# Layer 3's forward transform recorded in a fixed order of all engines, with products one group ahead, channels innermost, and other slots for layer 2

## The chip, the core and the metric

The kernel runs on one core of a Trainium2 chip. The metric is the device time of one execution in microseconds (us), from the first to the last instruction. The engines are named as the profile names them: PE multiplies matrices, PEld is its loading of weights (it runs beside PE), DVE works on vectors, ACT copies and applies functions, POOL is the general engine, SP issues most of the loads. SBUF is the memory that the engines read; PSUM takes the results of PE.

## The reference, cut to what matters

Four layers follow each other on x of 4 x 64 x 256 x 256 (images, channels, rows, columns), each of them x + f(norm(x)) with a norm over groups of two channels. The change touches the last layer, and the slots in SBUF that layer 2 takes over from layer 1.

```python
# layer 3: a few Fourier modes of the normalized x, mixed over channels
x_ft = jnp.fft.rfft2(x)
top = jnp.einsum('bixy,ioxy->boxy', x_ft[:, :, :M1, :M2], w1)       # M1 = M2 = 16
bot = jnp.einsum('bixy,ioxy->boxy', x_ft[:, :, H - M1:, :M2], w2)
out_ft = jnp.zeros((B, Co, H, Wf), dtype=x_ft.dtype)
out_ft = out_ft.at[:, :, :M1, :M2].set(top)
out_ft = out_ft.at[:, :, H - M1:, :M2].set(bot)
return jnp.fft.irfft2(out_ft, s=(H, W))

# ... cut: layers 0 to 2
x = x + _L1_conv_ref(_gn(x), L1_conv_kernel)      # 3x3 convolution
x = x + _L2_conv_ref(_gn(x), ...)                 # differences to neighbours, mask, two products
x = x + _L3_conv_ref(_gn(x), L3_conv_weights1, L3_conv_weights2)
```

## The kernel before

All data are float32. Three kinds of slots of one size (`y0`, `y1`, `y2`, two buffers each) live through all layers. Each is 11 x 258 floats in each of 128 partitions, and each layer takes them in its own way.

```python
def slot(self, k, name):
    return self.slots.tile([128, 11, self.W + 2], F32, tag=f"y{k}", name=name)
```

Layer 1 keeps its input tiles in `y0` and `y1` in turn, and its two normalized tiles in `y2`. Its loop, all engines in recorded order:

```python
xns = [self.slot(2, f"xn1_{k}")[:, 0:10] for k in range(2)]
# ... in load(n):
x = xt[n] = self.slot(n % 2, f"x1_{n}")[:, 0:10, 0:W]
# ... in normalize(n):
x, xn = xt.pop(n), xns[n % 2]
# ... the loop, NI = 64 blocks of 16 rows
for n in range(NI):
    load(n + 3)
    product(n, 1)
    fetch(n)
    product(n, 2)
    finish(n - 1)
    transform(n + 1, 1, 2)
    middle(n)
    product(n, 0)
    result(n, 0)
    transform(n + 1, 0, 3)
    normalize(n + 2)
    product(n, 3)
    result(n, 3)
    self.next_norms()
    ts.pop(n)
finish(NI - 1)
```

`normalize` is an ACT operation (line 256, `xn <- x, nb, r`), `fetch` an ACT copy (line 860, `s <- m`), `transform` are DVE operations (line 842, `t <- xn`), `middle` and `result` are DVE sums (lines 866 and 872), and `finish` takes sums for the next norm on ACT (lines 884 and 888, `junk <- o`).

Layer 2 begins with its slots and its first loads; block n, half g takes the input slot ((2n + g) mod 3) mod 2 and the normalized tile (2n + g) mod 3:

```python
xns = [self.slot(k, f"xn2_{k}_{i}")[:, 0:10] for i, k in enumerate((1, 2, 2))]
z = p_z.tile([128, 2, 10, W + 2], F32, name="z")
for t in xns + [z[:, 0], z[:, 1]]:
    nc.gpsimd.memset(t[:, :, 0 : W + 2 : W1], 0.0)
its = [(b, r0) for b in range(B) for r0 in range(0, H, 32)]
# ... cut
def load(n, g, s, ins=None):
    if n >= NI:
        return
    b, r0 = its[n]
    if s == 0:
        xt[n, g] = self.slot(((2 * n + g) % 3) % 2, f"x2_{n}_{g}")[:, 0:10, 0:W]
    top = r0 + 16 * g + 8 * s - 1
    i0, i1 = max(0, -top), min(10, H - top)
    d = nc.sync.dma_start(xt[n, g][halves[s], i0:i1], src[b][:, top + i0 : top + i1, :])
    if ins:
        self.after(d, ins)
for n, g in ((0, 0), (0, 1), (1, 0)):
    for s in range(2):
        load(n, g, s)
# ... cut: constants, then load_r (line 1004): the residual rows, eight loads each
```

The forward part of layer 3 takes four channels of an image at a time (a group, 1.05 MB, one load into a slot). It multiplies along the rows (`psa`), copies the result to SBUF on ACT (`a`), transposes it on PE (`psat`), and collects it with DVE in `ah`. After 16 groups of an image it multiplies along the width (`psx`), copies (`xw`), transposes again (`psxt`), and spreads the result over `xm`, scaled by the norm:

```python
for b in range(B):
    ah = p_ah.tile([128, NW, C, 4 * M], F32, tag="ah", name=f"ah_{b}")
    for c0 in range(0, C, CC):
        x = first.pop(c0, None) if b == 0 else None
        x = xs[b, c0] = x or load(b, c0, f"x3_{b}_{c0}")
        for c1 in range(0, CC, 4):
            ps = ps_a.tile([128, 2, W], F32, tag="a", name=f"psa_{b}_{c0}_{c1}")
            for n in range(NH):
                for j in range(2):
                    nc.tensor.matmul(
                        ps[halves[j]], eh[:, n, :], x[:, c1 + 2 * j : c1 + 2 * j + 2, n, :],
                        start=(n == 0), stop=(n == NH - 1),
                    )
            m = p_a.tile([128, 2, W], F32, tag="m", name=f"a_{b}_{c0}_{c1}")
            nc.scalar.copy(m, ps)
            pt = ps_t.tile([128, NW, 2, 2, 4 * M], F32, tag="t", name=f"psat_{b}_{c0}_{c1}")
            for n in range(NW):
                for k in range(2):
                    nc.tensor.transpose(
                        pt[:, n, k].rearrange("p j f -> p (j f)"),
                        m[:, k, n * 128 : (n + 1) * 128], self.ident,
                    )
            c = c0 + c1
            for n in range(NW):
                nc.vector.tensor_copy(
                    ah[:, n, c : c + 4, :].rearrange("p (j k) f -> p k j f", j=2), pt[:, n]
                )
        if c0 % 16 == 0:
            self.next_norms()
    if b < 3:
        load_w(b * NK)
    psx = ps_x.tile([128, 4, 128], F32, tag="x", name=f"psx_{b}")
    ahv = ah.rearrange("p n c (s g k r) -> p n g r k s c", s=2, g=4, k=4)
    for n in range(NW):
        for ri in range(2):
            for g in range(4):
                nc.tensor.matmul(
                    psx[32 * g : 32 * g + 32].rearrange("p k (s c) -> p k s c", s=2),
                    ew[:, n, ri, :], ahv[:, n, g, ri],
                    start=(n == 0 and ri == 0), stop=(n == NW - 1 and ri == 1),
                    tile_position=(0, 32 * g),
                )
    xw = p_a.tile([128, 4, 128], F32, tag="m", name=f"xw_{b}")
    nc.scalar.copy(xw, psx)
    pxt = ps_x.tile([128, 2, 4, 4, 2, M], F32, tag="xt", name=f"psxt_{b}")
    for s in range(2):
        for k in range(4):
            for h in halves:
                nc.tensor.matmul(
                    pxt[h, s, k].rearrange("p g r w -> p (g r w)"), xw[:, k, s * C : (s + 1) * C],
                    self.ident, start=True, stop=True,
                )
    r, nb = self.r[3][:, b : b + 1], self.nb[3][:, b : b + 1]
    up, low = halves
    for s in range(2):
        xb = xm[:, s, :, :, :, b].rearrange("p (g k) w r -> p k g w r", g=4)
        for k in range(4):
            v = pxt[:, s, k].rearrange("p g r w -> p g w r")
            nc.vector.tensor_scalar(xb[up, k], v[up], r[up], None, ALU.mult)
            nc.vector.tensor_scalar(xb[low, k, :, :, 0], v[low, :, :, 1], r[low], -1.0, ALU.mult, ALU.mult)
            nc.vector.tensor_scalar(xb[low, k, :, :, 1], v[low, :, :, 0], r[low], None, ALU.mult)
    for k, h in enumerate(halves):
        dc = xm[h, 0, 0, 0, k, b : b + 1]
        nc.vector.scalar_tensor_tensor(dc, nb[h], float(H * W), dc, ALU.mult, ALU.add)
```

Here the scheduler chooses the order of instructions on each engine. After that follow the mixing of the modes (`psm <- xm, wt`, line 1325, 1024 short PE records, weights in eight loads of 2.1 MB, of which `load_w` above starts the first three) and the inverse part (loads of x again, products, sums, stores).

Of the kernel before, what the change touches and what calls it, by code (L numbers as in the profile page):

```python
# [118 lines left out]
class _Net:  # L119
# [812 lines left out]
    def _layer2(self, ctx, src, dst):  # L932
# [18 lines left out]
        xns = [self.slot(k, f"xn2_{k}_{i}")[:, 0:10] for i, k in enumerate((1, 2, 2))]  # L951
        z = p_z.tile([128, 2, 10, W + 2], F32, name="z")
        for t in xns + [z[:, 0], z[:, 1]]:
            nc.gpsimd.memset(t[:, :, 0 : W + 2 : W1], 0.0)
# [16 lines left out]
        for n, g in ((0, 0), (0, 1), (1, 0)):  # L971
            for s in range(2):
                load(n, g, s)
        ones = cp.tile([128, Q], F32, name="ones")
# [227 lines left out]
    def _layer3(self, ctx, src, dst):  # L1202
# [33 lines left out]
        with ExitStack() as c2:  # L1236
# [11 lines left out]
            for b in range(B):  # L1248

                ah = p_ah.tile([128, NW, C, 4 * M], F32, tag="ah", name=f"ah_{b}")  # L1250
                for c0 in range(0, C, CC):
                    x = first.pop(c0, None) if b == 0 else None
                    x = xs[b, c0] = x or load(b, c0, f"x3_{b}_{c0}")
                    for c1 in range(0, CC, 4):
                        ps = ps_a.tile([128, 2, W], F32, tag="a", name=f"psa_{b}_{c0}_{c1}")
                        for n in range(NH):
                            for j in range(2):
                                nc.tensor.matmul(  # L1258
                                    ps[halves[j]], eh[:, n, :], x[:, c1 + 2 * j : c1 + 2 * j + 2, n, :],
                                    start=(n == 0), stop=(n == NH - 1),  # L1260
                                )
                        m = p_a.tile([128, 2, W], F32, tag="m", name=f"a_{b}_{c0}_{c1}")
                        nc.scalar.copy(m, ps)  # L1263
                        pt = ps_t.tile([128, NW, 2, 2, 4 * M], F32, tag="t", name=f"psat_{b}_{c0}_{c1}")
                        for n in range(NW):
                            for k in range(2):
                                nc.tensor.transpose(  # L1267
                                    pt[:, n, k].rearrange("p j f -> p (j f)"),
                                    m[:, k, n * 128 : (n + 1) * 128], self.ident,
                                )  # L1270
                        c = c0 + c1
                        for n in range(NW):
                            nc.vector.tensor_copy(
                                ah[:, n, c : c + 4, :].rearrange("p (j k) f -> p k j f", j=2), pt[:, n]
                            )
                    if c0 % 16 == 0:
                        self.next_norms()
                if b < 3:
                    load_w(b * NK)

                psx = ps_x.tile([128, 4, 128], F32, tag="x", name=f"psx_{b}")
                ahv = ah.rearrange("p n c (s g k r) -> p n g r k s c", s=2, g=4, k=4)
                for n in range(NW):
                    for ri in range(2):
                        for g in range(4):
                            nc.tensor.matmul(  # L1286
                                psx[32 * g : 32 * g + 32].rearrange("p k (s c) -> p k s c", s=2),
                                ew[:, n, ri, :], ahv[:, n, g, ri],
                                start=(n == 0 and ri == 0), stop=(n == NW - 1 and ri == 1),
                                tile_position=(0, 32 * g),  # L1290
                            )
                xw = p_a.tile([128, 4, 128], F32, tag="m", name=f"xw_{b}")
                nc.scalar.copy(xw, psx)

                pxt = ps_x.tile([128, 2, 4, 4, 2, M], F32, tag="xt", name=f"psxt_{b}")
                for s in range(2):
                    for k in range(4):
                        for h in halves:
                            nc.tensor.matmul(
                                pxt[h, s, k].rearrange("p g r w -> p (g r w)"), xw[:, k, s * C : (s + 1) * C],  # L1300
                                self.ident, start=True, stop=True,
                            )
                r, nb = self.r[3][:, b : b + 1], self.nb[3][:, b : b + 1]
                up, low = halves
                for s in range(2):
                    xb = xm[:, s, :, :, :, b].rearrange("p (g k) w r -> p k g w r", g=4)
                    for k in range(4):
                        v = pxt[:, s, k].rearrange("p g r w -> p g w r")
                        nc.vector.tensor_scalar(xb[up, k], v[up], r[up], None, ALU.mult)
                        nc.vector.tensor_scalar(xb[low, k, :, :, 0], v[low, :, :, 1], r[low], -1.0, ALU.mult, ALU.mult)  # L1310
                        nc.vector.tensor_scalar(xb[low, k, :, :, 1], v[low, :, :, 0], r[low], None, ALU.mult)
                for k, h in enumerate(halves):
                    dc = xm[h, 0, 0, 0, k, b : b + 1]
                    nc.vector.scalar_tensor_tensor(dc, nb[h], float(H * W), dc, ALU.mult, ALU.add)

# [101 lines left out]
```

## Time and profile before

The time is 7476.2 us, the median of three runs (7473.46 to 7483.11). The profiled execution has a span of 7469.9 us.

| stretch (us from the start) | what runs | PE busy | DVE busy | ACT busy | DMA, GB/s |
|---|---|---|---|---|---|
| 5500 to 5530 | from layer 1 to layer 2 | 12.38 of 30 | 14.16 | 16.83 | 109 |
| 5540 to 6830 | layer 2 | 1256.04 of 1290 | 1117.42 | 1001.31 | 171 |
| 6841 to 7093 | layer 3, forward | 197.41 of 252 | 80.83 | 39.69 | 255 |
| 7093 to 7149 | layer 3, mixing | 54.79 of 56 | 4.00 | 6.04 | 190 |
| 7149 to 7470 | layer 3, inverse | 266.03 of 321 | 179.85 | 38.68 | 399 |

How to read the profile: the page sums over the whole execution, so a stage of 250 us hardly shows in it. The busy time by stretch is the view to start with. The timeline then lists instructions in order of time: start, duration, engine, line of the kernel, output and inputs, how many were merged, and in square brackets how long the engine stood idle before it and what it waited for. A product of float32 operands appears as two PE records, a transpose as one. SPq is the queue of SP, with the loads that it issues. A row that a fence shows is a row of the view, word for word, and "..." stands for rows left out.

### The profile page before, as it was taken

What the parts mean: (1) busy time and instruction counts of PE and PEld (TensorE: products, weight loads), DVE (VectorE), ACT (ScalarE), POOL (GpSimd) and SP (SyncE); (2) the same over time, 40 slices, a digit from 0 to 9 for tenths busy, and PEclk for the clock granted to TensorE, in tenths of its full rate; (3) what the DMA queues carried; (4) which work ended last, traced back from release to release, by engine and by line L of the source; (5) the groups of instructions that cost most, each with busy time, mean ns of one, the idle gap of its engine ahead of it and who ended that gap; (6) DMA issues with size and microseconds to landing.
All of it is one profiled execution on the core that took longest, in us unless ns stands there. A gap on an engine that the chain in (4) does not pass through costs nothing. (4 is left out here: it accounts for less than half of the span.)

```text
span 7469.9 us, 396764 instructions
## 1 busy us (share of the span) xinstructions
PE 7164.3 (96%) x188280; PEld 4283.8 (57%) x188280; DVE 6440.8 (86%) x5705; ACT 3917.9 (52%) x4173; POOL 658.6 (9%) x1435
## 2 busy tenths in 40 slices
PE   6999999999999999999999999899989999998797
PEld 4666666666666666666666666533334444443275
DVE  7999999999999999999999999889979889885345
ACT  3444444444554444454445445377768877773111
POOL 0000000000000000000000000011102222221011
PEclk9999999999999999999999999999999999999955
DMA  3222222222222222222111111399967666667689
GB/s 131 63 64 63 62 63 61 59 63 62 60 62 60 60 63 63 60 61 57 46 46 47 47 46 48 76 223 228 229 149 181 172 178 175 172 173 235 239 350 393
DMA packets 651193, 875.49 MB, mean 117 GB/s; under 512 B 44020, under 2 KB 470212, under 8 KB 647524
## 3 DMA queue, kind: packets, MB, share of 16 engines
q1 hardware_dynamic: 568548, 581.61, 29.0%
q0 software_dynamic: 81024, 268.50, 12.4%
q8 instruction: 1477, 24.20, 1.4%
q14 instruction: 144, 1.18, 0.1%
HBM read 581.50 MB, written 268.44 MB: 114 GB/s over the span
## 5 line engine op out<-in xcount | busy, mean ns | idle before, releaser
L482 PE MATMUL psd<-y,diag 32*32 32x512 f32 x73296 | 2526.3, 597 | 8.0 <-issue 7.6
L520 DVE SCALAR_TENSOR_TENSOR v<-y,sb_w_dw,v 128x2048 f32<-128x2048 f32 x1024 | 2391.5, 2335 | 112.3 <-ACT v L518 89.3
L482 PEld LDWEIGHTS psd<-y,diag 32*32 32x32 f32 x73296 | 1534.6, 103 | 837.3 <-issue 309.9
L462 ACT COPY y<-psy 128x512 f32<-128x512 f32 x1536 | 916.8, 661 | 1671.0 <-PE psy L455 1669.6
L420 DVE TENSOR_TENSOR up<-psu,flt 128x768 f32<-128x768 f32 x1024 | 933.0, 952 | 210.0 <-PE psu L417 209.5
L455 PEld LDWEIGHTS psy<-sb_c_bdft,up 64*64 64x64 f32 x49152 | 855.2, 135 | 340.4 <-issue 127.0
L455 PE MATMUL psy<-sb_c_bdft,up 64*64 64x64 f32 x49152 | 925.0, 221 | 22.8 <-issue 19.5
L417 PE MATMUL psu<-win,xf 64*64 64x384 f32 x8192 | 788.5, 489 | 23.3 <-DVE h L502 10.5
L1038 DVE TENSOR_TENSOR q<-xn 128x2313 f32<-128x2313 f32 (+2 forms) x256 | 628.0, 2496 | 1.7 <-ACT xn L256 1.7
L1093 PE MATMUL one<-z,wp 32*32 32x512 f32 x16384 | 594.6, 597 | 17.6 <-issue 13.1
L1039 ACT ACTIVATE q<-q 128x2313 f32<-128x2313 f32 (+2 forms) x256 | 529.1, 2086 | 32.2 <-DVE q L1038 30.9
L496 ACT ACTIVATE h<-psd 128x1024 f32<-128x1024 f32 x258 | 250.6, 1023 | 516.4 <-PE psd L482 516.4
L256 ACT ACTIVATE xn<-x,nb,r 128x1024 f32<-128x1024 f32 (+3 forms) x272 | 487.1, 1794 | 28.3 <-DMA x<-x 24.4
L1093 PEld LDWEIGHTS one<-z,wp 32*32 32x32 f32 x16384 | 366.9, 103 | 226.4 <-issue 84.6
L1052 PE MATMUL div<-q,ones 64*32 64x512 f32 x8192 | 468.6, 598 | 13.7 <-ACT q L1039 9.8
L427 POOL MEMSET y<- 128x22 f32 x384 | 51.8, 136 | 4212.2 <-ACT y L435 3204.1
L417 PEld LDWEIGHTS psu<-win,xf 64*64 64x64 f32 x8192 | 302.3, 135 | 193.1 <-issue 88.7
L1126 POOL DMA_DIRECT2D x<-r x512 | 273.5, 541 | 971.4 <-DVE r L1123 880.9
L852 PE MATMUL m<-t,wk 64*64 64x512 f32 x3072 | 341.1, 588 | 0.0
L1052 PEld LDWEIGHTS div<-q,ones 64*32 64x32 f32 x8192 | 154.1, 107 | 321.8 <-issue 257.8
L535 DVE TENSOR_TENSOR v<-g,v 64x1024 f32<-64x1024 f32 x257 | 313.5, 1220 | 9.3 <-ACT g L528 1.4
L502 DVE TENSOR_TENSOR h<-h,psd 128x1024 f32<-128x1024 f32 x258 | 302.7, 1215 | 6.1 <-PE psd L482 5.7
(154 smaller groups left out, 7403.2 us busy)
## 6 DMA issues: line engine op xcount, KB each, us to landing
x<-x SPq DMA_DIRECT2D x240, 640.0 KB, 6.6
x<-x SPq DMA_DIRECT2D x122, 1024.0 KB, 10.5
x<-in_x_dram SPq DMA_DIRECT2D x256, 256.0 KB, 3.7
x<-o POOLq DMA_DIRECT2D x128, 512.0 KB, 8.0
r<-x SPq DMA_DIRECT2D x512, 128.0 KB, 4.0
x<-r POOLq DMA_DIRECT2D x512, 128.0 KB, 3.8
out_dram<-x POOLq DMA_DIRECT2D x64, 1024.0 KB, 10.0
r<-in_x_dram SPq DMA_DIRECT2D x248, 256.0 KB, 3.8
```

Of the source, the lines that this page charges most:

```text
L256: self.nc.scalar.activation(dst, src, AF.Identity, bias=self.nb[n][p0:p1, b : b + 1], scale=self.r[n][p0:p1, b : b + 1])
L417: nc.tensor.matmul(ps[halves[n], s, 0:384], xf[t][halves[s], n, 4 * g + k], win[halves[s]], start=True, stop=True)
L420: nc.vector.tensor_mul(ups[t, g][:, :, k, :], ps[:, :, 0:384], flt.broadcast_to([128, 2, 384]))
L455: nc.tensor.matmul(ps[halves[c], n, s, :, k, :], up[halves[n], s, k, i * 128 + c * C : i * 128 + (c + 1) * C], bdft[halves[n]], start=True ...
L462: nc.scalar.copy(yt[t][i][:, 3:11, w0 : w0 + 64].rearrange("p r (k n w) -> p n r k w", k=4, n=2), ps[:, :, s])
L482: ins = nc.tensor.matmul(d[q // 2][quarters[j], q % 2], diag[quarters[q], i, k, :], rows_in(t, i, quarters[q], j, dy)[:, :, dx : dx + W], ...
L520: nc.vector.scalar_tensor_tensor(v, s, wdw[:, 2, k : k + 1], v, ALU.mult, ALU.add)
L852: nc.tensor.matmul(rows2(m)[halves[j], s], w[dx][halves[s]], ts[n][halves[s], i, 2 * j : 2 * j + 2, dx : dx + W], start=(dx == 0), stop=(d ...
L1038: nc.vector.tensor_sub(d, p0, p1)
L1039: nc.scalar.activation(d, d, AF.Square)
L1052: ins = nc.tensor.matmul(ps[quarters[j], h], ones[halves[h]], q[n, g, k][halves[h], r + 2 * j : r + 2 * j + 2, o : o + W], start=(m == 0), ...
L1093: ins = nc.tensor.matmul(rows2(ps[g])[quarters[j], k], w[quarters[i]], z[quarters[i], h, 2 * j + dy : 2 * j + dy + 2, dx : dx + W], tile_p ...
```

## The change

Layer 3's forward part is recorded in a fixed order on PE, DVE, ACT and SP. The products of group i stand ahead of the transposes of group i - 1, so that PE has work while ACT copies. Where an image ends, the products along the width come after the products of the second group of the next image. `ah` has its channels innermost, so that the products along the width read neighbouring floats; the DVE copies into it now write with a step. The second transposes are laid out so that six DVE operations an image spread the result, where 24 did. The three weight loads stand at fixed places, each after the last x load of an image. Layer 2 makes its loads ahead of its normalized tiles and takes `y2`, `y2`, `y1` for those, where it took `y1`, `y2`, `y2`. The amount of products and of loaded bytes stays the same.

```diff
-        xns = [self.slot(k, f"xn2_{k}_{i}")[:, 0:10] for i, k in enumerate((1, 2, 2))]
         z = p_z.tile([128, 2, 10, W + 2], F32, name="z")
-        for t in xns + [z[:, 0], z[:, 1]]:
-            nc.gpsimd.memset(t[:, :, 0 : W + 2 : W1], 0.0)
 ... cut
         for n, g in ((0, 0), (0, 1), (1, 0)):
             for s in range(2):
                 load(n, g, s)
+        xns = [self.slot(k, f"xn2_{i}")[:, 0:10] for i, k in enumerate((2, 2, 1))]
+        for t in xns + [z[:, 0], z[:, 1]]:
+            nc.gpsimd.memset(t[:, :, 0 : W + 2 : W1], 0.0)
 ... cut: layer 3; the old loop goes out as it is printed above
+            ah_of = lambda b: ahs[b].rearrange("p n (s g k r) c -> p n g r k s c", s=2, g=4, k=4)
+            def along_h(b, c0):
+ ... cut: the load of x and the products psa, as before
+                m = ms[b, c0] = p_a.tile([128, 2, W], F32, tag="m", name=f"a_{b}_{c0}")
+                nc.scalar.copy(m, ps)
+            def turned(b, c0):
+                if c0 == 0:
+                    ahs[b] = p_ah.tile([128, NW, 4 * M, C], F32, tag="ah", name=f"ah_{b}")
+ ... cut: the transposes psat, as before
+                for n in range(NW):
+                    nc.vector.tensor_copy(
+                        ahs[b][:, n, :, c0 : c0 + 4].rearrange("p f (j k) -> p k j f", j=2), pt[:, n]
+                    )
+                if c0 % 16 == 0:
+                    self.next_norms()
+            def along_w(b):
+ ... cut: the products psx, reading ah_of(b)[:, n, g, ri], and the copy xw, as before
+            def spread(b):
+                pxt = ps_x.tile([128, 2, 4, 4, 2 * M], F32, tag="xt", name=f"psxt_{b}")
+                for s in range(2):
+                    for k in range(4):
+                        for h in halves:
+                            nc.tensor.matmul(
+                                pxt[h, s, :, k], xw[:, k, s * C : (s + 1) * C], self.ident, start=True, stop=True
+                            )
+                for s in range(2):
+                    xb = xm[:, s, :, :, :, b]
+                    v = pxt[:, s].rearrange("p g k (r w) -> p (g k) w r", r=2)
+                    nc.vector.tensor_scalar(xb[up], v[up], r[up], None, ALU.mult)
+                    nc.vector.tensor_scalar(xb[low, :, :, 0], v[low, :, :, 1], r[low], -1.0, ALU.mult, ALU.mult)
+                    nc.vector.tensor_scalar(xb[low, :, :, 1], v[low, :, :, 0], r[low], None, ALU.mult)
+ ... cut
+            with tc.manual_schedule(engines={PE, DVE, Activation, SP}):   # names cut
+                for i in range(len(groups) + 2):
+                    if i < len(groups):
+                        along_h(*groups[i])
+                    b, k = divmod(i - 1, NG)
+                    if b > 0 and k == 0:
+                        along_w(b - 1)
+                    if 0 < i <= len(groups):
+                        turned(*groups[i - 1])
+                    if b > 0 and k == 0:
+                        spread(b - 1)
+                    if i % NG == NG - 1 and i // NG < 3:
+                        load_w(i // NG * NK)
```

## The prediction

> **What bounds the kernel now.** I read the page first, then the busy time by stretch, then the timeline and the chain of waits inside the stretches that the change touches. The page says TensorE is busy 96% of 7469.9 us, but the change touches little of that, so the average is no guide; the stage is. Layer 3 starts at about 6830 us, and its stretches read (busy us of PE, weight load, DVE, ACT and POOL; then the TensorE clock, DMA share and GB/s):
>
> ```profile
> 6841.00:7093.00 252.00, 197.41 (x1008) 70.33 (x1008) 80.83 (x232) 39.69 (x68) 0.00 (x0) 0.98 0.72 255
> 7093.00:7149.00 56.00, 54.79 (x1024) 54.73 (x1024) 4.00 (x16) 6.04 (x16) 0.00 (x0) 0.50 0.49 190
> 7149.00:7470.00 321.00, 266.03 (x1408) 204.07 (x1408) 179.85 (x289) 38.68 (x64) 48.22 (x64) 0.56 1.01 399
> ```
>
> The first is the forward part (252 us), the second the mixing of modes (56 us), the third the inverse part (321 us, DMA share 1.01 at 399 GB/s: bound by transfers, and not changed). Only the forward part has slack: no engine and no DMA is full in it. Its timeline over one group of four channels shows why:
>
> ```profile
> 6854.33 0.58 ACT L1263 COPY a<-psa 128x512 f32<-128x512 f32 x1 [2.66 <-PE psa L1258]
> 6854.97 0.66 PE L1267 MATMUL psat<-sb_c_ident,a 128*128 128x128 f32 x4 [0.72 <-ACT a L1263]
> 6855.55 0.20 PEld L1258 LDWEIGHTS psa<-x,sb_c_eh 128*64 128x64 f32 x4 [0.17 <-issue]
> 6855.55 1.94 PE L1258 MATMUL psa<-x,sb_c_eh 128*64 128x512 f32 x8
> 6857.57 0.58 ACT L1263 COPY a<-psa 128x512 f32<-128x512 f32 x1 [2.66 <-PE psa L1258]
> ```
>
> It is a ring: products, ACT copy, transposes, next products. From copy to copy is 6857.57 - 6854.33 = 3.24 us, and 0.72 of it PE stands still for the copy. Loads keep pace with that, 1.05 MB per 3.24 us = 324 GB/s, until the step along the width, where six filled slots leave nothing to load. Two five-microsecond stretches show the DMA empty there, and full later, when a 2.1 MB weight load has put the x loads behind:
>
> ```profile
> 6895.00:6900.00 5.00, 5.00 (x28) 0.65 (x16) 0.00 (x0) 0.56 (x1) 0.00 (x0) 1.00 0.00 1
> 7005.00:7010.00 5.00, 4.24 (x20) 1.19 (x16) 1.40 (x4) 0.58 (x1) 0.00 (x0) 1.00 1.05 387
> ```
>
> The end of the forward part is serial. The timeline of it, and beside it a product of layer 2 for comparison:
>
> ```profile
> 6796.98 7.10 PE L1052 MATMUL div<-q,ones 64*32 64x512 f32 x128
> ...
> 7074.67 7.06 PE L1286 MATMUL psx<-ah,ew 128*32 128x512 f32 x32 [0.52 <-DVE ah L1273]
> 7082.47 1.97 PE L1299 MATMUL psxt<-sb_c_ident,xw 128*64 128x128 f32 x32 [0.75 <-ACT xw L1293]
> 7084.49 0.43 DVE L1309 TENSOR_SCALAR xm<-psxt,r 64x128 f32<-64x128 f32 x1 [9.55 <-PE psxt L1299]
> ```
>
> Layer 2's 128 records ran eight tiles abreast: 7.10 / 16 = 0.44 us a step. The 32 records of psx, four tiles abreast, make 8 steps, so 7.06 / 8 = 0.88 us each, twice as long, though both stream 512 columns. The difference I see is that psx reads channels 64 elements apart.
>
> The last place is far earlier, where layer 1 ends and layer 2 begins. Timelines of the load queue and of ACT:
>
> ```profile
> 5481.46 13.15 SPq L1004 DMA_DIRECT2D r<-x  x8
> 5494.72 3.99 SPq L967 DMA_DIRECT2D x<-x  x2
> ```
> ```profile
> 5506.49 2.52 ACT L256 ACTIVATE xn<-x,nb,r 128x2560 f32<-128x2560 f32 x1 [16.12 <-DMA x<-x]
> 5508.92 1.09 ACT L860 ACTIVATE s<-m,i 128x1024 f32<-128x1024 f32 x1
> 5514.30 1.12 ACT L860 ACTIVATE s<-m,i 128x1024 f32<-128x1024 f32 x1 [0.27 <-PE m L852]
> ```
>
> ACT waits 16.12 us for layer 2's second x tile, whose load stands behind eight residual loads, and layer 1's last two copies (s) stand behind ACT. PE is busy only 0.49 us between 5500 and 5510.
>
> **What the Trainium skill says.** "SBUF — State Buffer", the section "SBUF: two separate sides", gives SBUF lines of 16 bytes that need two hits each for full rate; a 256-byte step would have one. The factor of two above agrees. "DMA: Bandwidth & Descriptors", Bandwidth, gives 341 GB/s for a 1 MB transfer alone and 425 for 16 MB[...]. Here it is 324 when paced and 387 when several loads stand in the queue. "TensorE: Matmul & The Clock Gate", What's actually happening, says that the clock halves after an idle window of about 3.4 us; here PE stops at 7084.4 and the clock is 0.50 from about 7090.
>
> **The change, part by part.**
>
> 1. *Products ahead of the transposes.* A group no longer waits for its copy. On PE eight product records at 0.427 us a pair (the weight loads in the timeline stand 0.43 us apart) are 1.71 us; four transposes, from the row "psat x8, 1.02 us" in the chain, are 0.51. Sum 2.22, with gaps 2.25 us against 3.24. So PE alone could do 64 groups in 144 us. But 1.05 MB per 2.25 us is 466 GB/s, which no stretch reaches. The loads become the bound: at 390 GB/s 2.69 us a group, at 345 3.04.
>
> 2. *Channels innermost.* psx at full rate: 32 records in 8 steps of 0.44 = 3.5 instead of 7.06 us, 3.5 us saved per image. For images 0 to 2 that now lies beside the loads; only the last counts. The DVE copies to ah write single floats 256 bytes apart and may go from 0.416 to about 0.55 us: two in a group are 1.1 us, well below 2.7, so nothing.
>
> 3. *Fewer DVE operations in the spread.* 24 become 6. Rows for 128 and 64 elements are 440 and 340 ns, a line of 240 ns + 1.56 ns per element. So 512 elements 1.04 us and 256 0.64: 2 x (1.04 + 2 x 0.64) = 4.6 us instead of 8.3 (7084.5 to 7092.8). Again 3.7 us counts once, at the end.
>
> 4. *Weights.* The queue of before put two 2.1 MB weight loads ahead, at 6828 and 6836, and one inside. Now all three come inside: 4.2 MB, 10.8 us, more for the loads. In return the stores of layer 2, for which the first ACT copy waits until 6841.57, share the DMA with less: I take 6840.
>
> The forward part by its loads: eight groups are there or in flight before the third product. Load 8 is issued when that product has run, about 6844 (its clock is still low). Then 56 x 1.049 + 3 x 2.097 = 65.0 MB. At 390 GB/s that is 167 us, plus 2 to land: 7013. At 345 it is 188: 7034. I take 375: 173, so 7019. Tail: last products 1.7, copy 0.6, transposes 0.7, DVE copies 1.1, psx 3.5 + 0.3, copy 0.6, psxt 2.0, spread 4.6 = 15.1, some of it within the landing: 7033. Before, mixing started at 7093.0. Saved: **60 us** (66 at 390, 45 at 345).
>
> 5. *Layer 2's slots.* The x tile (0,1) now takes the buffer that layer 1 frees at about 5469.5, and in the order of the changed program its load stands ahead of (1,0), (1,1) and the residual loads; it lands long before use. Layer 2's first normalized tile instead takes layer 1's own buffer, so ACT must wait for DVE's transform of block 62, which ends at 5491.2; with the border memsets 5492.0, then 2.8 us for the normalization: s of block 62 at 5494.8, where it was 5508.92. The second tile waits for the transform of block 63 (s + 6.9 = 5501.7) and delays the last s to 5504.4, where it was 5514.30. From there DVE's sums and ACT's statistics run as before, but ACT ends at 5514.5 instead of 5527.5, for the last sums are held less by PE. Layer 2's constants hang on that end. Saved: **13 us** (10 if only the last s counts, 14 if only the one before).
>
> 6. *Mixing.* Its 1024 short PE records take 54.8 us at a clock of 0.50. The gap ahead of them shrinks from 8.6 us (7084.4 to 7093.0) to about 5, so the first few may run at full clock: **2 us** at the most, 1 taken. The inverse part keeps its 321 us.
>
> Sum: 60 + 13 + 1 = 74 us. 7476 - 74 = 7402; I say 7402.
>
> **Rivals.** *The loads give back nothing:* a single load's rate stays near 345 GB/s even with six in the queue. For it: the stretches of refill after the first image's width step show 331 to 370. Against: the stretch above and its neighbours show 385 to 410 with only x loads left. Then 45 saved instead of 60: 7417. *PE is the bound, not the loads:* if loads ran at 410 to 430 GB/s, the forward part would end at about 6998 + 14, 80 us saved: 7382. *The fixed order brings a new wait:* spread holds DVE for 4.6 us ahead of the next copies and both transpose buffers fill, or a small norm product waits on DVE in the middle of PE's order. Each is at most 2 us per image and lies in the shadow of six loaded groups; if they add up, 7415. *The layer 1 gain is hidden:* layer 2 might start only when the residual loads, now behind (1,1), have landed. They are issued from about 5495 and the constants wait for ACT at 5514, so I think not; if so, 7412.
>
> **Range and chances.** The load rate moves the time by 15 to 20 us, the transition by 5, a new wait by 10 to 15. I give 7382 to 7430. A gain of 2% would need 7326.7, 149 us: more than the whole slack of the forward part. A loss would need a stall that nothing shows.
>
> **What would show it.** Right: copy to copy about 2.7 us in the forward part, DMA share near 1.0 all through it, PE's waits there on x, not on the ACT copy; psx in about 3.5 us; six spread operations in under 5; mixing starting about 73 us earlier; no long wait of ACT near 5490. Wrong: a DMA share below 0.9, psx still at 7 us (then the step in the read was not its cause), DVE copies above 1.1 us each, or a wait at the layer 1 border in another place.

## The result, and the profile after

The changed kernel takes 7414.16 us, the median of four runs (7402.0 to 7427.63); the kernel before has 7478.82 (7473.46 to 7483.11, four runs). The ratio is 0.9914, with a 95% interval of 0.9896 to 0.9933: 0.9% less. The profiled executions are 7399.9 and 7469.9 us long, 70.0 apart.

Whole times of one kernel wander by 20 us and more from run to run, and the kernel before has medians from 7463.64 to 7520.39 us on the chips used below. So the parts are compared as stages, each measured in the trace from one first start to the next. This table was worked out from the timelines of the two profiled executions (us):

| stage | before | after | difference |
|---|---|---|---|
| layer 1, first product to layer 2's first product (psz) | 685.8 | 674.9 | -10.9 |
| layer 2, to layer 3's first product (psa) | 1297.8 | 1295.4 | -2.4 |
| from there to layer 3's first ACT copy (a) | 11.5 | 12.1 | +0.6 |
| forward part, to the first mixing product (psm) | 251.5 | 193.8 | -57.7 |
| mixing, to the first product of the inverse part (pst) | 56.3 | 56.4 | +0.1 |
| inverse part, to the end | 320.5 | 318.2 | -2.3 |

The rows sum to -72.6; ahead of layer 1's first product, where the code is the same, the kernel after is 2.6 us longer in this profile.

Over all programs that ran, layer 2, unchanged, lay between 1290 and 1309 us and the inverse part between 318 and 322; their differences are scatter. The forward part of the changed kernel was profiled twice: 193.8 and 194.5.

The busy time by stretch of the kernel after, for the forward part, the mixing and the inverse part, with the columns as before (PE, weight load, DVE, ACT, POOL; clock, DMA share, GB/s):

```profile
6831.00:7025.00 194.00, 179.81 (x1016) 69.99 (x1016) 88.29 (x169) 39.71 (x68) 1.09 (x2) 0.98 0.90 339
7025.00:7081.00 56.00, 54.79 (x1024) 54.70 (x1024) 4.20 (x17) 5.85 (x16) 0.00 (x0) 0.50 0.50 190
7081.00:7400.00 319.00, 272.66 (x1408) 211.91 (x1408) 179.97 (x289) 38.89 (x65) 48.23 (x64) 0.54 1.02 402
```

PE is now busy 179.81 of 194 us, where it had 197.41 of 252; the sum fell by 17.6, of which the faster psx explains 4 x 3.4 = 13.7. DMA share rose from 0.72 to 0.90. Both are high, so this view alone does not tell which one sets the pace. A stretch in the middle, one beside a weight load, and one near the end, from the same view:

```profile
6895.00:6900.00 5.00, 5.00 (x28) 1.85 (x26) 2.19 (x6) 1.17 (x2) 0.00 (x0) 1.00 1.05 388
6915.00:6920.00 5.00, 2.67 (x14) 1.06 (x12) 1.21 (x3) 0.58 (x1) 0.00 (x0) 0.86 1.04 385
7005.00:7010.00 5.00, 5.00 (x26) 1.85 (x26) 2.18 (x5) 1.18 (x3) 0.00 (x0) 1.00 0.05 20
```

In the first, PE and DMA are both full. In the second, PE falls to 2.67 of 5 while DMA stays full: there it waits for x. In the third, DMA is empty (0.05) and PE still full: the loads are done, and the products are not. The timeline of one group shows the new order:

```profile
6896.46 0.58 ACT L1264 COPY a<-psa 128x512 f32<-128x512 f32 x1 [1.87 <-PE psa L1259]
...
6896.87 1.94 PE L1259 MATMUL psa<-x,sb_c_eh 128*64 128x512 f32 x8
...
6898.74 0.66 PE L1274 MATMUL psat<-sb_c_ident,a 128*128 128x128 f32 x4
...
6898.91 0.59 ACT L1264 COPY a<-psa 128x512 f32<-128x512 f32 x1 [1.87 <-PE psa L1259]
...
6899.33 1.94 PE L1259 MATMUL psa<-x,sb_c_eh 128*64 128x512 f32 x8
```

The ring is open: no PE row has a wait in brackets. From copy to copy it is 6898.91 - 6896.46 = 2.45 us, where it was 3.24. Products take 6898.74 - 6896.87 = 1.87 us until the transposes start, and the transposes 6899.33 - 6898.74 = 0.59 until the next products start. The list of waits, from layer 3's start to the end of the forward part (waited for: us in total, times, longest), has one row of PE products and loads left:

```profile
PE psa L1259 <- DMA x<-x: 6.0, 4, 2.3
```

So in all the loads hold the products for 6.0 us. (The transposes have one wait of 7.44 us put down to x; it is the start, where they wait for the first copy.) The longest of the four waits costs more than itself, as the timeline of PE shows:

```profile
6918.90 3.46 PE L1259 MATMUL psa<-x,sb_c_eh 128*64 128x512 f32 x8 [2.33 <-DMA x<-x]
```

The eight records behind it take 3.46 us instead of 1.94, 1.5 more; the clock from 6919 to 6922 us is 0.50. Behind the waits of 1.52 and 2.00 us they take 1.94.

The timeline of the end of the forward part:

```profile
7013.82 3.64 PE L1290 MATMUL psx<-ah,ew 128*32 128x512 f32 x32 [0.74 <-DVE ah L1278]
...
7018.22 1.97 PE L1306 MATMUL psxt<-sb_c_ident,xw 128*64 128x128 f32 x32 [0.76 <-ACT xw L1297]
...
7020.24 1.10 DVE L1314 TENSOR_SCALAR xm<-psxt,r 64x512 f32<-64x512 f32 x1 [6.04 <-PE psxt L1306]
...
7025.30 1.88 PE L1351 MATMUL psm<-xm,wt 128*64 128x8 f32 x32 [5.11 <-DVE xm L1319]
```

psx takes 3.64 us instead of 7.06, and from the first spread operation to its end at 7024.9 it is 4.7 us instead of 8.3. At the border of layers 1 and 2, the timeline of ACT, and then that of the load queue:

```profile
5494.16 2.94 ACT L256 ACTIVATE xn<-x,nb,r 64x256 f32<-64x256 f32 x2 [1.05 <-POOL xn L973]
5497.00 1.09 ACT L860 ACTIVATE s<-m,i 128x1024 f32<-128x1024 f32 x1
...
5504.46 2.52 ACT L256 ACTIVATE xn<-x,nb,r 128x2560 f32<-128x2560 f32 x1 [2.34 <-POOL xn L973]
5506.88 1.09 ACT L860 ACTIVATE s<-m,i 128x1024 f32<-128x1024 f32 x1
...
5514.92 1.91 ACT L884 ACTIVATE junk<-o 128x2048 f32<-128x2048 f32 x1 [2.93 <-DVE o L872]
```
```profile
5461.96 36.78 SPq L964 DMA_DIRECT2D x<-x  x8
5498.78 10.98 SPq L1004 DMA_DIRECT2D r<-x  x8
```

The x loads now stand ahead of the residual loads in the queue, and ACT's 16.12 us wait has become waits of 1.05 and 2.34 us, both put down to POOL's border memsets, which follow DVE's transform of the tile that used the slot.

### The profile page after: what moved, and what is told of

It reads as the page before. It is cut to its first block, busy times and chain, and to the rows that moved or that the text cites. A ratio compares the mean times of both kernels' runs of the same rounds, so it can differ in the third digit from the quotient of the medians.

```text
span 7399.9 us, 396694 instructions
## 1 busy us (share of the span) xinstructions
PE 7151.1 (97%) x188280; PEld 4272.4 (58%) x188280; DVE 6444.7 (87%) x5633; ACT 3917.4 (53%) x4173; POOL 658.8 (9%) x1435
## 5 line engine op out<-in xcount | busy, mean ns | idle before, releaser
L420 DVE TENSOR_TENSOR up<-psu,flt 128x768 f32<-128x768 f32 x1024 | 932.5, 952 | 204.5 <-PE psu L417 203.9
L1093 PE MATMUL one<-z,wp 32*32 32x512 f32 x16384 | 593.3, 598 | 17.8 <-issue 13.5
L1052 PE MATMUL div<-q,ones 64*32 64x512 f32 x8192 | 467.8, 596 | 12.1 <-ACT q L1039 9.3
```

The source lines that it names most:

```text
L420: nc.vector.tensor_mul(ups[t, g][:, :, k, :], ps[:, :, 0:384], flt.broadcast_to([128, 2, 384]))
L1052: ins = nc.tensor.matmul(ps[quarters[j], h], ones[halves[h]], q[n, g, k][halves[h], r + 2 * j : r + 2 * j + 2, o : o + W], start=(m == 0), ...
L1093: ins = nc.tensor.matmul(rows2(ps[g])[quarters[j], k], w[quarters[i]], z[quarters[i], h, 2 * j + dy : 2 * j + dy + 2, dx : dx + W], tile_p ...
```

## The experiments

Two theories stood against each other once the result was known. **Loads**: the transfers set the pace of the forward part, as the prediction had it. **PE**: its own 2.45 us a group do. Under the first, what PE is spared beside the loads is worth nothing; under the second it counts in full, group by group and image by image. All figures below named "stage" are the forward part (first ACT copy to first mixing product), to be read against 193.8 unless said otherwise; "start gap" is the row above it in the table, against 12.1.

### One part alone: layer 2's slots

The kernel before, with the new order of loads and slots of layer 2 and nothing else:

```diff
-        xns = [self.slot(k, f"xn2_{k}_{i}")[:, 0:10] for i, k in enumerate((1, 2, 2))]
         ... the loads
+        xns = [self.slot(k, f"xn2_{i}")[:, 0:10] for i, k in enumerate((2, 2, 1))]
```

> The kernel before with layer 2's slots and the place of its loads changed, layer 3 as before. Theory: ACT's 16.1 us wait for layer 2's second x tile goes, two waits of 1 to 2.5 us for DVE's transforms come, and layer 2's first product starts 11 us earlier, measured from the same point of layer 1; the whole time falls by 10 to 13 us. Rival: layer 2 waits later for its residual loads, which now stand behind one more x tile, and gives it back: within 3 us of before.

Measured: 7448.47 us, ratio 0.9974 (0.9966 to 0.9982). Layer 1's stage is 674.4 us, 11.4 less than before and the same as after (674.9), and the forward part keeps its 251.2. So the gain at this border belongs to the slots and the order of the loads, which were not tried apart, and does not overlap with the rest. The timed ratio is worth 0.26% or 19 us (13 to 25 by its interval; the medians on this chip are 15 apart), more than the stage's 11.4; what the rest is is not attributed.

### Undo the lead of the products

```diff
-                    b, k = divmod(i - 1, NG)
+                    b, k = divmod(i, NG)
                     if b > 0 and k == 0: along_w(b - 1)
-                    if 0 < i <= len(groups): turned(*groups[i - 1])
                     if b > 0 and k == 0: spread(b - 1)
+                    if i < len(groups): turned(*groups[i])
```

> The changed kernel, but the transposes of a group stand directly behind its own products, in the same fixed order. Theory (the lead over the copy is what counts): copy to copy goes back from 2.45 to 3.25 us, 64 x 0.8 = 51 us; since the width step is shorter and the spread too, the forward part from its first ACT copy to the first mixing product is 235 to 245 us instead of 193.8. Rival (fixing the order is what counts, whatever the order): below 205 us. Rival (loads set the pace at 2.7 us): 193.8 + 64 x 0.55 at the most, 215 to 230.

Measured: 7433.67 us, ratio 0.9961 (0.9947 to 0.9975); stage 237.5, 43.7 more than after. Its timeline:

```profile
6895.69 0.58 ACT L1264 COPY a<-psa 128x512 f32<-128x512 f32 x1 [2.62 <-PE psa L1259]
...
6896.33 0.66 PE L1274 MATMUL psat<-sb_c_ident,a 128*128 128x128 f32 x4 [0.69 <-ACT a L1264]
...
6896.91 1.94 PE L1259 MATMUL psa<-x,sb_c_eh 128*64 128x512 f32 x8
...
6898.95 0.58 ACT L1264 COPY a<-psa 128x512 f32<-128x512 f32 x1 [2.68 <-PE psa L1259]
```

The ring is back: 0.69 us of PE's time in front of the transposes, and 6898.95 - 6895.69 = 3.26 us a group. In the changed kernel a group without a wait takes 2.455 us. Over 64 groups 3.26 - 2.455 is 51.5 us; the 6.0 us that PE waits for loads only in the changed kernel, and the 1.5 us of slow clock behind one of these waits, bring it to 44.0, near the 43.7. The lead is the largest part of the change.

### Undo the order of channels

```diff
-ahs[b] = p_ah.tile([128, NW, 4 * M, C], F32, tag="ah", name=f"ah_{b}")
+ahs[b] = p_ah.tile([128, NW, C, 4 * M], F32, tag="ah", name=f"ah_{b}")
```

The reads in psx and the DVE copies go with it, as they were before.

> The changed kernel with ah laid out as before (channels outermost). Theory where PE sets the pace: each image's products along the width take 7.0 instead of 3.6 us, 3.4 us times four images, 13 to 14 us in all; the DVE copies go back from 0.60 to 0.42 us and give nothing. Theory where the loads set the pace: only the last image's 3.4 us show, since the others lie beside loads, 3 to 5 us. If the step in the read is not the cause of the slow products, they stay at 3.6 us and nothing changes.

Measured: 7402.82 us, ratio 0.9916 (0.9901 to 0.9931), which the timed runs cannot tell from the changed kernel. The stage can: 203.9, 10.1 more. The tile view of psx and ah (duration in ns: min/median/max, then first and last start):

```profile
L1290 PE MATMUL psx<-ah,ew x128: 1024/1035/1042, 6866.1 to 7016.8; 128*32 128x512 f32 x128
```
```profile
L1278 DVE COPY ah<-psat x128: 411/415/425, 6823.5 to 7010.6; 128x256 f32<-128x256 f32 x128
```

The same view of the kernel after:

```profile
L1290 PE MATMUL psx<-ah,ew x128: 592/592/617, 6876.0 to 7016.9; 128*32 128x512 f32 x128
```
```profile
L1278 DVE COPY ah<-psat x128: 572/602/618, 6833.3 to 7013.6; 128x256 f32<-128x256 f32 x128
```

The step in the read is the cause of the slow psx: one edit takes a record from 592 to 1035 ns, with the same 512 columns. The price is DVE's copy, 602 ns instead of 415, which delays next to nothing (the last psx waits 0.7 us for it, and 0.5 here). The last image's psx alone would be worth 7.06 - 3.64 = 3.4 us. The stage moved by 10.1, three times that. The images in the middle therefore count too, and that speaks against Loads. It is less than the 13 to 14 us that the PE theory said, because PE, slower here, waits less for loads: four times 3.4 is 13.7, the waits on x in this run's list are 3.9 us where they were 6.0, and the 1.5 us of slow clock do not occur. 13.7 - 2.1 - 1.5 is 10.1.

### Take half of the bytes away

This kernel leaves out half of each x load of the forward part: two of the four channels of a group, and the products read the other two twice. Groups that the inverse part uses again, and the first six, are loaded whole. PE, ACT and DVE do as much as before.

```diff
-                x = xs[b, c0] = x or load(b, c0, f"x3_{b}_{c0}")
+                x = xs[b, c0] = x or load(
+                    b, c0, f"x3_{b}_{c0}", n_c=CC if (b == B - 1 and c0 >= C - NX * CC) else CC // 2
+                )
-                            ps[halves[j]], eh[:, n, :], x[:, 2 * j : 2 * j + 2, n, :],
+                            ps[halves[j]], eh[:, n, :], x[:, 0:2, n, :],
```

> The changed kernel with two of four channels loaded for the groups of the forward part that the inverse part does not use again; the products read those two twice, so that PE does the same work. It leaves out the other two channels' data. Theory where the loads set the pace: 54 of 65 MB become half, the forward part becomes shorter by 20 us or more, until PE sets the pace. Theory where PE sets the pace (2.455 us a group, 5.00 of 5.00 us busy in most stretches of the changed kernel): only the few waits for x go, each after a weight load: 5 to 9 us, and DMA share falls to about 0.55.

Measured: 7376.08 us, ratio 0.9881 (0.9866 to 0.9896); stage 185.9, only 7.9 less. The forward part by stretch:

```profile
6819.00:7005.00 186.00, 177.98 (x1016) 69.19 (x1016) 88.44 (x169) 39.70 (x68) 1.09 (x2) 0.98 0.59 210
```

DMA share is down to 0.59 and 210 GB/s, and PE works 177.98 of 186 us. If the loads had set the pace, a stage with so much less to load would have lost 20 us or more. It lost the 6.0 us of waits on x, of which none are left in its list, the 1.5 us of slow clock, and 0.4. **Loads** falls: they cost a few microseconds beside weight loads, and PE is the bound.

### Undo the place of the weight loads

```diff
-                    if i % NG == NG - 1 and i // NG < 3:
-                        load_w(i // NG * NK)
+                    if i == len(groups) - 1:
+                        for k in range(3): load_w(k * NK)
```

> The changed kernel with its three early weight loads behind the last x load of the forward part. PE sets the pace by now (half the loads gave only 7.9 us), so only PE's waits for x behind each weight load go: the forward part from the first ACT copy to the first mixing product is 186 to 189 instead of 193.8 us. If the weights had to be early, the first mixing product would wait for its weight and the part would be 195 us or more. If loads set the pace after all: 178 us.

Measured: 7410.79 us, ratio 0.9893 (0.9878 to 0.9908); stage 186.0, 7.8 less, and no wait of products on x is left in the list. The weights land behind the last x load and still before mixing needs them. So the 6.0 us of waits, and the 1.5 us of slow clock behind one of them, came from these three loads; their place in the changed kernel costs 7.8 us.

### Pools in another order

The start gap remained. The first ACT copy writes the buffer of `a`, and its pool lies where layer 2's last residual rows are, so it waits until their stores have read them. The start in the timeline of the kernel after:

```profile
6819.37 5.35 PE L1259 MATMUL psa<-x,sb_c_eh 128*64 128x512 f32 x16 [2.50 <-DVE sel L1118]
...
6831.52 1.07 ACT L1264 COPY a<-psa 128x512 f32<-128x512 f32 x2 [23.11 <-DMA x<-x]
```

The products of two groups are done by 6824.7 and ACT copies only at 6831.5. The row names loads (x<-x); in the second profile of the same kernel the same wait, 22.8 us, is put down to layer 2's stores (x<-r). Here the weights' pool, not needed for a long time, is allocated behind `ah` and `a` and so takes that place:

```diff
-            p_w = pool(c2, "l3w", 3)
             p_ah, p_a = pool(c2, "l3ah", 1), pool(c2, "l3a", 3)
+            p_w = pool(c2, "l3w", 3)
```

> The changed kernel with the pool of the weights allocated after those of ah and a, so that a no longer lies where layer 2 keeps its last residual rows. Theory: the first ACT copy waits only for memory that the last stores of layer 2 still read; with another place it follows the first products by 3 us instead of 12.1, and the time falls by 9 us. Rival: the copy waits for something else that lands then (the constants, the image's norm), and the gap stays at 12 us. Rival: the gap goes but the loads, which could not be issued ahead, give it back later as waits on x: forward part longer than 198 us.

Measured: 7413.65 us, ratio 0.9901 (0.9884 to 0.9917). The gap goes from 12.1 to 3.2 us; the stage goes up to 196.9, so 3.1 of the 8.9 are given back. What is left, 5.8 us, lies within the scatter of the timed runs. In its timeline and its list of waits:

```profile
6822.27 0.59 ACT L1264 COPY a<-psa 128x512 f32<-128x512 f32 x1 [14.60 <-PE psa L1259]
6824.43 0.59 ACT L1264 COPY a<-psa 128x512 f32<-128x512 f32 x1 [1.58 <-PE psa L1259]
```
```profile
PE psa L1259 <- DMA x<-x: 8.1, 4, 3.8
```

ACT now waits for its products alone. The earlier start makes the products use up the loaded groups earlier, and the waits on x grow from 6.0 to 8.1 us; two of them now have slow products behind them, where one had.

### Both together

> Both of the last two together. If they are independent, the gap ahead of the first copy is 3 us and the forward part 187 to 190 us: 13 to 16 us less than the changed kernel. If the loads become the bound once PE starts earlier, the sum of both stretches stays above 197 us.

Measured, with the two edits above: 7401.73 us, ratio 0.9881 (0.9866 to 0.9896). Gap 3.4 and stage 184.7: 188.1 together, where the changed kernel has 205.9 and the kernel before 263.0. With the weights last, the earlier start is kept whole: 17.8 us less, slightly more than 8.9 + 7.8.

### Leave the order to the scheduler

The changed code, with the scheduler choosing the order on each engine:

```diff
-            with tc.manual_schedule(engines={PE, DVE, Activation, SP}):   # names cut
+            if True:
```

> The changed kernel, the same program order, but without the fixed order: the scheduler places the instructions. It keeps the products one group ahead of the transposes nearly everywhere. Theory (the lead counts, not who fixes it): forward part 190 to 200 us. Rival (the fixed order is needed): above 215 us, with waits on the ACT copy.

Measured: 7444.64 us, ratio 0.9942 (0.9927 to 0.9957); stage 217.1, 23.3 more. From its timeline, and from its list of waits over layer 3's forward part:

```profile
6911.91 1.94 PE L1259 MATMUL psa<-x,sb_c_eh 128*64 128x512 f32 x8
...
6914.59 0.66 PE L1274 MATMUL psat<-sb_c_ident,a 128*128 128x128 f32 x4 [0.74 <-ACT a L1264]
...
6915.18 1.94 PE L1259 MATMUL psa<-x,sb_c_eh 128*64 128x512 f32 x8
```
```profile
PE psat L1274 <- ACT a L1264: 25.6, 39, 0.7
```

In 39 places PE still waits for the copy, 25.6 us in sum; 33 of the waits are the full 0.74 us. The stage lost a little less than that. It is not the lead alone: the scheduler also put two of the three weight loads ahead of the stage again (at 6830 and 6835 us), so that the 6.0 us of waits on x are gone, and it mixed the products along the width into those of the next group. What the mixing costs was not tried alone. The code offers the lead; the scheduler's order uses it in full for fewer than half of the 64 groups. Both the code and the fixed order are needed.

### Undo the spread

The second transposes and the 24 small operations as before, within the new order (a single run).

```diff
-                pxt = ps_x.tile([128, 2, 4, 4, 2 * M], F32, tag="xt", name=f"psxt_{b}")
+                pxt = ps_x.tile([128, 2, 4, 4, 2, M], F32, tag="xt", name=f"psxt_{b}")
+ ... the transposes and the 24 operations as in the kernel before
```

> The changed kernel with the spread in 24 DVE operations again, and the second transposes laid out as before. Theory: the last image's spread takes 8.3 instead of 4.6 us and the other three lie beside PE's work, so the forward part is 197 to 198 us instead of 193.8. Rival: for the other images too the spread holds up DVE's copies of the next groups until both transpose buffers are full: 2 us more for each, 202 to 205 us.

Measured: 7462.75 us in its single run, on a chip where the kernel before has 7520.39; stage 206.5, 12.7 more than 193.8 and 11.9 more than the 194.6 of the changed kernel on the same chip; both are above the 202 to 205 that the rival said. The place after an image, in its timeline, and a row of its list of waits:

```profile
6936.94 0.32 DVE L1321 SCALAR_TENSOR_TENSOR xm<-nb,xm 64x1 f32<-64x1 f32 x2
6937.27 2.84 DVE L1278 COPY ah<-psat 128x256 f32<-128x256 f32 x6
...
6938.44 0.63 PE L1274 MATMUL psat<-sb_c_ident,a 128*128 128x128 f32 x4 [3.07 <-DVE ah L1278]
```
```profile
PE psat L1274 <- DVE ah L1278: 9.2, 3, 3.1
```

With 24 operations DVE is held for some 8.5 us. Both transpose buffers fill meanwhile, DVE catches up with six copies in a row, and PE waits 3.07 us. That happens three times, 9.2 us; the last image adds 8.3 - 4.7 = 3.6 us. The sum, 12.8, is near the 11.9, but the account is not closed: the waits on x fall from 6.3 to 3.6 us, and behind two of the waits of 3.07 us the products of a group take 3.21 and 2.90 us instead of 1.94. With six operations the changed kernel has no such wait.

### Fewer changes between products and transposes

The 2.455 us a group hold more than the products and transposes themselves, and the suspicion was the change from products to transposes and back. Here groups go in pairs, on top of the two edits of pools and weights: products of two groups, then transposes of the two groups before, with five buffers for `a` instead of three. The same chip ran the changed kernel again, and pools and weights again.

```diff
-                for i in range(len(groups) + 2):
-                    if i < len(groups): along_h(*groups[i])
+                for p in range(len(groups) // 2 + 2):
+                    for i in (2 * p, 2 * p + 1):
+                        if i < len(groups): along_h(*groups[i])
 ...
-                    if 0 < i <= len(groups): turned(*groups[i - 1])
+                    for i in (2 * p - 2, 2 * p - 1):
+                        if 0 <= i < len(groups): turned(*groups[i])
```

> The changed kernel as it is, beside the two versions that go further, for a comparison on one chip. From the first products of layer 3 to the first mixing product 204 to 208 us, as in its first profile (205.9). Ratio to before 0.989 to 0.993.

> The version with other pools and late weights, and the products of two groups followed by the transposes of the two groups before them (five buffers for a instead of three). Theory: of 2.455 us a group only 1.71 + 0.43 are streaming, 0.31 are the two changes between products and transposes, and half as many changes save 0.16 us a group, 10 us: from the first products to the first mixing product 177 to 181 us instead of 188.1. Rival: at 2.30 us a group the loads, 2.69 us each at 390 GB/s, bind at last, and PE waits for x: 183 to 188 us with waits on x in the trace.

> The version with other pools and late weights once more, beside the changed kernel on one chip: 187 to 190 us from the first products to the first mixing product, 16 to 19 us less than the changed kernel, 0.2% of the whole.

Measured, with the kernel before at 7520.39 us on this chip:

| kernel | time, us | ratio to before (95%) | gap + stage |
|---|---|---|---|
| after, again | 7449.87 | 0.9905 (0.9889 to 0.9920) | 11.1 + 194.6 |
| pools and weights, again | 7434.76 | 0.9887 (0.9871 to 0.9904) | 3.3 + 184.7 |
| pairs | 7426.13 | 0.9878 (0.9857 to 0.9898) | 3.1 + 180.2 |

The timeline of a pair in the middle of the forward part:

```profile
6868.84 3.65 PE L1259 MATMUL psa<-x,sb_c_eh 128*64 128x512 f32 x16
...
6872.43 1.09 PE L1274 MATMUL psat<-sb_c_ident,a 128*128 128x128 f32 x8
...
6873.45 3.65 PE L1259 MATMUL psa<-x,sb_c_eh 128*64 128x512 f32 x16
```

A pair takes 6873.45 - 6868.84 = 4.61 us, 2.305 a group. The two kernels give the cost of a change: 16 products take 3.59 us until the transposes start and 8 take 1.87, so 8 of them are 1.72 and a change is 0.15; 8 transposes take 1.02 and 4 take 0.585, so four are 0.435 and a change is again 0.15. Two changes a group cost 0.30, and pairs halve that. Over 64 groups that is 10 us; the stage fell by 4.5 (184.7 to 180.2), and gap and stage together, 183.3, lie where the rival put them (183 to 188) and not where the theory did (177 to 181). The longest stretch between start and tail shows why:

```profile
6905.00:7022.00 117.00, 116.04 (x710) 48.87 (x706) 56.49 (x111) 26.98 (x46) 0.00 (x0) 1.00 1.05 392
```

DMA share is 1.05 at 392 GB/s for 117 us on end, with PE at 116.04. PE and loads are now both full. Of the 10 us some 3 come back as waits of PE in the list: 1.7 on x, 1.0 on DVE's copies and 0.8 on ACT's, where pools and weights alone have 0.2 in all. Where the rest went is not settled; a longer start and tail of a pair are candidates. On this chip, pairs with the two other edits are 23.7 us below the changed kernel and the lowest of all kernels that do the whole computation. Its interval overlaps that of pools and weights alone.

## Why the prediction was right, and where it was not

7402 us were predicted (7382 to 7430) and 7414.16 measured; 74 saved against 70.0 in the profiled pair and 64.7 in the medians. The stage of the forward part was to be 193 us (7033 - 6840) and is 193.8. That the number fits does not mean that its reason did: in the forward part, luck had a share in it.

1. *Products ahead.* The direction and the size of the lead are right. **The step that failed is "the loads become the bound".** PE was put at 2.25 us a group and the loads at 2.69 or more; PE takes 2.455 and the loads hold it for 6.0 us in all. Mis-sized was PE's term: 1.71 + 0.51 and gaps of 0.03, where the runs show 1.72 + 0.435 + two changes of 0.15. The term of the loads was right as a rate: from 6845 to 7000 us they ran at 394 GB/s. At that rate 1.05 MB take 2.66 us, more than 2.455. But a group is the wrong unit: psx and psxt hold PE for some 5.6 us more an image, and up to six groups stand loaded ahead. So an image of 16 groups takes PE 16 x 2.455 + 5.6 = 44.9 us and the loads 16 x 2.66 = 42.6, and only the 5.3 us of a weight load put the loads behind. By PE: from the transposes of group 1 (start 6836.77) to those of group 62 (7011.61) are 61 x 2.455 = 149.8, three steps along the width 17, waits on x 6.0: 172.8 of the 174.8 us, and 1.5 of the rest are the slow clock behind one wait. The rival "PE is the bound" named the bound, but for loads at 410 to 430 GB/s, where they ran at 394, and with PE's 2.25 us, hence too large a gain (80 us).

2. *Channels innermost.* The size is right: psx 3.64 for 3.5 us, DVE's copy 0.602 for 0.55. That only the last image counts was wrong, since it followed from step 1: undone, it costs 10.1 us and not 3.5. The Trainium skill's reason ("SBUF — State Buffer", SBUF: two separate sides) agrees again: a read step of 256 bytes gives 1035 ns and a step of 4 bytes 592.

3. *Spread.* 4.6 us predicted, 4.7 measured. Counted once again, where it is worth 11.9 to 12.7 with the fixed order, because 24 operations would have brought just the wait that a rival named: it was put at 2 us an image and is 3 with the old spread, and with the new one it isn't there.

4. *Weights.* 10.8 us were put on the two loads that are added inside; all three moved behind the x loads give back 7.8. The second half, "the stores share the DMA with less, 6840", failed: the gap from first product to first copy is 12.1 instead of 11.5 us. The run with other pools shows that this wait hangs on the place of the buffer, which the change leaves as it was.

The four parts, each undone alone, sum to 43.7 + 10.1 + 12.7 - 7.8 = 58.7, against 57.7 measured; so close a sum is not more than a sign, since each part undone also takes away waits on x. The prediction came to nearly the same sum with two errors against each other: images counted too little, PE's group too short. That they nearly cancel is luck.

5. *Layer 2's slots.* 13 us predicted, 10.9 measured (11.4 alone). The first product of layer 1 stands 2.6 us later in this trace; with that taken off, the two s copies start at 5494.4 and 5504.3, predicted 5494.8 and 5504.4. What failed is the end: ACT was to be done at 5514.5, and is at 5516.4, because the last sums wait 2.93 us for DVE. The rival that layer 2 waits for the late residual loads is not seen.

6. *Mixing.* No gain, where 1 us was taken. PE stops 5.1 us in front of it, and the clock is 0.50 over all of it. The Trainium skill ("TensorE: Matmul & The Clock Gate", What's actually happening) halves the clock after an idle window of about 3.4 us, one that runs freely and does not begin with the gap. This trace shows less than that to be enough: behind the wait of 2.33 us the clock was 0.50, behind the one of 2.00 us it was 1.00. So 5.1 us were no reason to expect a full clock; that it falls after every gap of that length is not shown.

The signs named for wrong and right: copy to copy 2.45 us (2.7 said), DMA share 0.90 over the stage (1.0 said), and waits of PE on the copy gone, as said, but few on x. The first two were the sign that PE sets the pace.

The load rates of the Trainium skill ("DMA: Bandwidth & Descriptors", Bandwidth: 341 GB/s for 1 MB, 425 for 16 MB) bracket what the runs show: 392 to 394 GB/s over the long stretches in which loads stand in the queue without a gap. The page's table, for loads that POOL issues, varies the size of a transfer; the number of loads in the queue is varied alone neither there nor in a run here.

## What to carry to other kernels

If removing a wait brings one resource to its limit, work out the two rates that remain to a tenth of a microsecond, over the whole cycle that repeats (here an image, not a group) and with the changes between kinds of work in them, before saying which of them is the bound: saved work elsewhere counts fully or not at all by that answer. A matching total is no proof; one run that halves the suspected load costs a line and settled it here. And look at where the next stage's first buffer lies: a wait of 9 us for the last stage's stores went away by allocating two pools in another order.

## What the runs showed that was not expected

A change between products with 64-column weights and transposes with 128-column ones costs PE about 0.15 us each way (from pairs against single groups), 19 us over this stage; what in the change takes the time is not shown. A write step of 256 bytes costs DVE a factor of 602/415 = 1.45 for 256 floats from PSUM, a read step of 256 bytes costs PE 1035/592 = 1.75 in the record, and nearly two in the time of a whole psx (7.06 to 3.64 us). The scheduler's order lost the lead of one group in 39 of 64 places, in 33 of them fully. A wait of 2.33 us made the eight records behind it take 3.46 us instead of 1.94. And full DMA share (1.05) and full PE stood side by side for 117 us with almost no wait between them, so that neither figure names the bound by itself.
